# A woven graph-attention layer: VectorE adds up all three products of every slot group from the 22nd tile on, and two hand-set pacings are taken out

## The chip, the cores and the metric

The kernel runs on one core of a Trainium2 chip. The metric is device time in microseconds of one execution, from the median of several. Before the change it is 1743.26 us (three runs, 1741.64 to 1750.56 us). All profile lines below come from one profiled execution, whose own run took 1741.64 us and whose trace spans 1739.8 us from the first to the last instruction; the granted TensorE clock was 0.985 of full speed over that span.

## What is computed

One layer of graph attention over 4096 nodes with 512 features and 8 heads of 64, followed by a feed-forward block and a last layer norm. The mask is an adjacency matrix in which a node has some 17 neighbours, so nearly all of the 4096 x 4096 scores are masked out.

```python
hs, ht = layer_norm(x), layer_norm(h_target)
q = (ht @ Wq + bq).reshape(T, H, HD) / sqrt(HD)
k, v = (hs @ Wk + bk), (hs @ Wv + bv)            # per head
logits = where(adj != 0, q . k, -1e30)
ctx = softmax(logits) @ v
ht = layer_norm(ht + ctx @ Wo + bo)
out = layer_norm(x + ht + gelu(ht @ W1) @ W2)
```

Everything is float32. `adj` is 4096 x 4096 int32.

## The kernel before

**Preparation (to about 280 us).** K and V of all nodes are computed and written to one table in HBM (`kvd`, 1024 numbers per node). VectorE and ScalarE turn the rows of `adj` into lists of neighbours. The nodes are then sorted by their number of neighbours, in two halves, so that a tile of 128 nodes has nodes of about the same count.

**Tiles and slot groups.** There are 32 tiles. A tile's cap (11 to 39) is the largest number of neighbours that a node of it has. The caps in the order of the work are 11, 13, 14, 15, 15, 16, 17, 17, 18, 19, 19, 20, 22, 23, 24, 39, 12, 38, 13, 24, 14, 23, 15, 22, 15, 20, 16, 19, 17, 18, 17, 18: "tile 21" is the 22nd of them. Each neighbour position is a slot. Slots are worked on three at a time (`S = 3`); three slots are a full slot group, and a tile may end in a smaller one. 211 groups in all.

**One slot group.** GpSimd issues one gather per slot from `kvd` (L994) into a ring of 20 slots. VectorE multiplies the keys with the query (L1287) and sums by head (L1293). ScalarE takes the exponential (L1300, L1315) and multiplies the third slot's v with its weight, head by head (L1265, L1268). VectorE multiplies the first two slots' v with their weights (L1234). From tile 9 on it adds the second product to the first (L1238), and from tile 21 on (`DENSE = 21`) it also adds the third, but only in every other full group, by `j0 // S % 2` (L1241). What has not been added up goes to TensorE slot by slot: four 128x128 transposes per slot (L1247), which accumulate the context in PSUM (`cps`). So a slot added up by VectorE is four transposes less.

**A tile's tail.** `finish(i, ...)` is a generator that `advance()` steps twice per slot group. It sums the weights, takes the reciprocal, lets ScalarE spread it (L1133), TensorE transpose it (L1139), VectorE scale the context (L1144), TensorE add the residual (L1153) and multiply with Wo (L1157), and then goes through the layer norm to the transposed `h2T` (L1188, L1192). Between these stand `yield`s, whose number is set by `slow`: with `slow = 0` one step lies between L1144 and L1157, with `slow = 1` four. `slow` is 1 for tiles 7 to 10.

**A tile's front.** Gather of `h_target`, normalisation, transposes (L1037), query product (L1047), then VectorE's scaling of the query (L1052).

**Feed-forward.** `feed(g)` works on pairs of tiles (18 groups; the first three and the last are single tiles). It sleeps until `h2T` of its group is there, then goes through W1 (L1407), gelu (L1410) and W2 (L1416). `end` does the last norm, with rstd by GpSimd's pow (L692, called from `power`).

**The order of the work** is not left to a scheduler. `_weave` runs four generators (attention, the feeds, the second half's lists, weight loads), and always takes a piece from the one whose clock is lowest; a piece adds its cost in planner units to its clock. A pair of tiles costs 60 units in attention (`cost * n` twice per slot group) and 60 in the feed. `PACE` multiplies the cost of attention for some groups: 0.7 for tiles 1 to 4, 0.85 for tiles 5 to 8, 0.9 for tiles 9 and 10, and 1.1 for tiles 11 to 18. Every engine then works in the order in which its instructions were laid down.

Of the kernel before, what the change touches and what calls it, by code (L numbers as in the profile page):

```python
# [443 lines left out]
def adj_resnorm_kernel(  # L444
# [58 lines left out]
    S = 3  # L503
# [29 lines left out]
    with tc.tile_pool(name="keep", bufs=1) as keep:  # L533
# [17 lines left out]
        with ExitStack() as late:  # L551
# [171 lines left out]
            def behind(ins):  # L723
                return tc.issue_after(ins[-1]) if ins else nullcontext()
# [349 lines left out]
            def step(gens, i):  # L1074

                if i in gens and next(gens[i], StopIteration) is StopIteration:
                    del gens[i]

            def request(k):


                while issued[0] <= min(k + AHEAD, len(SG) - 1):
                    issue(issued[0])
                    mine = set(range(place[issued[0]], place[issued[0]] + SG[issued[0]][2]))
                    for m in range(max(k - len(held_up), 0), issued[0]):
                        assert not mine & set(range(place[m], place[m] + SG[m][2]))
                    issued[0] += 1
# [28 lines left out]
            def finish(i, p, cps, group, hs, mv):  # L1116


                rec, tq, cap = recs[i], tqs.pop(i), TILES[i][1]
                slow = 0 if i < QUICK or i > 10 else 1  # L1120
                first = i == 0

                nc.vector.scalar_tensor_tensor(p[:, :cap, :], rec[:, E0:E0 + cap].unsqueeze(2)
# [72 lines left out]
            def go_on():  # L1196
                for i in list(fronts):
                    step(fronts, i)
# [18 lines left out]
            def attention():  # L1217


                tails, pend, turns = [], [], []  # L1220

                def advance():
                    go_on()
                    for t in list(tails):
                        if next(t, StopIteration) is StopIteration:
                            tails.remove(t)

                def values(i, j0, n, kv, p, cps, after):

                    m = n - 1 if n == S else n
                    v4 = kv[:, :m, D:].rearrange("p j (h d) -> p j h d", h=H)
                    nc.vector.tensor_tensor(v4, v4, p[:, j0:j0 + m, :].unsqueeze(3)  # L1234
                                            .to_broadcast([P, m, H, HD]), ALU.mult)
                    slots = list(range(n))
                    if m > 1 and i >= ADDS and TILES[i][1] < (HEAVY if i > NA else 23):
                        nc.vector.tensor_add(kv[:, 0, D:], kv[:, 0, D:], kv[:, 1, D:])  # L1238
                        slots.remove(1)
                        if n == S and i >= DENSE and j0 // S % 2:  # L1240
                            nc.vector.tensor_add(kv[:, 0, D:], kv[:, 0, D:], kv[:, S - 1, D:])  # L1241
                            slots.remove(S - 1)

                    def turn():
                        for j in slots:
                            for c in range(KC):
                                nc.tensor.matmul(cps[:, c, :], kv[:, j, D + c * P:D + (c + 1) * P],  # L1247
                                                 ident, is_transpose=True,
                                                 start=j0 + j == 0 and c == 0,
                                                 stop=j0 + n == TILES[i][1] and j == slots[-1],  # L1250
                                                 skip_group_check=True)
                        if after is not None:
                            tails.append(after)

                    turns.append(turn)
                    held_up[:] = turns

                def add_up():
                    while turns:
                        turns.pop(0)()  # L1260
                    held_up.clear()

                def by_scalar(kv, lg):
                    pa = sp.tile([P, H], F32, name="pa")
                    nc.scalar.activation(pa, lg[:, S - 1, :], AF.Exp)  # L1265
                    for hd in range(H):
                        v = kv[:, S - 1, D + hd * HD:D + (hd + 1) * HD]
                        newest[:] = [nc.scalar.mul(v, v, pa[:, hd:hd + 1]).ins]  # L1268

                request(0)  # L1270
                yield 0.0
                k = 0
                for group in GROUPS:
                    hs = []
                    mv = sp.tile([P, 2, 2], F32, name="mv2")
                    cost = 0.5 * UNIT * len(group) / 2 / sum(TILES[i][1] for i in group)
                    if 0 < group[0] < 19:
                        cost *= PACE[(group[0] > 4) + (group[0] > 8) + (group[0] > 10)]
                    for i in group:
                        cps = ps.tile([P, KC, P], F32, name="cps", bufs=2)  # L1280
                        while k < len(SG) and SG[k][0] == i:
                            _, j0, n = SG[k]
                            while i not in tqs:
                                step(fronts, i)
                            kv, tq = kvs.pop(k), tqs[i]
                            with behind(closing[:1 if j0 < 2 * S else 2]):
                                nc.vector.tensor_tensor(kv[:, :n, :D], kv[:, :n, :D],  # L1287
                                                        tq[:, :D].unsqueeze(1)
                                                        .to_broadcast([P, n, D]), ALU.mult)
                            lg = sp.tile([P, S, H], F32, name="lg")  # L1290
                            latest[:] = [lg[:, 0, 0:1]]
                            with behind(closing if j0 == S else []):
                                logits[:] = [nc.vector.tensor_reduce(  # L1293
                                    lg[:, :n, :],
                                    kv[:, :n, :D].rearrange("p j (h d) -> p j h d", h=H),
                                    AX.X, ALU.add).ins]
                            if i != 1:
                                closing.clear()
                            if j0 > 0:
                                nc.scalar.activation(p[:, j0:j0 + n, :], lg[:, :n, :], AF.Exp)  # L1300
                            add_up()
                            if k > 0:
                                request(k - 1)
                            advance()
                            yield cost * n
                            if pend:
                                values(*pend.pop())
                                if i < QUICK:
                                    add_up()
                                if i < QUICK or i > NA:  # L1310
                                    request(k)
                            advance()
                            if j0 == 0:
                                p = sp.tile([P, MAXE, H], F32, name="p", bufs=1)
                                nc.scalar.activation(p[:, :n, :], lg[:, :n, :], AF.Exp)  # L1315
                            if n == S:
                                by_scalar(kv, lg)
                            last = j0 + n == TILES[i][1]
                            after = finish(i, p, cps, group, hs, mv) if last else None
                            pend.append((i, j0, n, kv, p, cps, after))  # L1320
                            yield cost * n
                            k += 1
                values(*pend.pop())
                add_up()
                while tails:
                    advance()
                    yield 3.0
                verdict()
# [138 lines left out]
            DENSE = 21  # L1467
            QUICK = 7
            UNIT = 60.0
            PACE = (0.7, 0.85, 0.9, 1.1)  # L1470

            ed = all_edges()
            steps = 2 * NQ + 1
# [41 lines left out]
            def fill():  # L1515
# [4 lines left out]
                for cost in _take(ed, FILL * steps):  # L1520
                    yield cost

            att = attention()
            _weave((projections(), 0), (prepare(), 0), (fill(), 0))
            src.close()
# [58 lines left out]
```

## Time and profile before

| what | value |
|---|---|
| median of 3 runs | 1743.26 us |
| the profiled execution, its own time | 1741.64 us |
| its span in the trace | 1739.8 us |
| TensorE (PE) busy | 1654.6 us, 95% |
| VectorE (DVE) busy | 1421.7 us, 82% |
| ScalarE (ACT) busy | 1236.4 us, 71% |
| GpSimd (POOL) busy | 994.5 us, 57% |
| first key product (L1287) of tile 0, 10, 21, 31 | 282.6, 646.5, 1183.2, 1600.2 us |
| last Wo product (L1157) ends | about 1658 us |

The page gives busy time by engine. A row of waits says which instruction of an engine was waiting for which other one, the microseconds in total, how often and the longest. A table of stretches gives each engine's busy time between two moments, and the clock granted to TensorE. A timeline row has start, length, engine, line, operation, out<-in, shape and count, and in brackets the idle time before it.

### The profile page before, as it was taken

What the parts mean: (1) busy time and instruction counts of PE and PEld (TensorE: products, weight loads), DVE (VectorE), ACT (ScalarE), POOL (GpSimd) and SP (SyncE); (2) the same over time, 40 slices, a digit from 0 to 9 for tenths busy, and PEclk for the clock granted to TensorE, in tenths of its full rate; (3) what the DMA queues carried; (4) which work ended last, traced back from release to release, by engine and by line L of the source; (5) the groups of instructions that cost most, each with busy time, mean ns of one, the idle gap of its engine ahead of it and who ended that gap; (6) DMA issues with size and microseconds to landing.
All of it is one profiled execution on the core that took longest, in us unless ns stands there. A gap on an engine that the chain in (4) does not pass through costs nothing. (4 is left out here: it accounts for less than half of the span.)

```text
span 1739.8 us, 22750 instructions
## 1 busy us (share of the span) xinstructions
PE 1654.6 (95%) x6994; PEld 1075.0 (62%) x6994; DVE 1421.7 (82%) x2450; ACT 1236.4 (71%) x3136; POOL 994.5 (57%) x824
## 2 busy tenths in 40 slices
PE   7999897899999999998999999999999999999997
PEld 3444444677676766665667677666656666666665
DVE  6887797889898999987778898898988879898700
ACT  5776674679678878786767877696877777686711
POOL 1000155666566685687777777777776776767101
PEclk9999998899999999999999999999999999999999
DMA  9999988978888898677788788778776777776100
GB/s 357 376 381 359 360 275 294 360 259 299 291 286 296 311 338 288 227 239 235 262 289 276 272 290 306 258 265 271 271 237 222 264 234 261 237 264 218 42 1 27
DMA packets 141611, 461.02 MB, mean 265 GB/s; under 512 B 18036, under 2 KB 23048, under 8 KB 141480
## 3 DMA queue, kind: packets, MB, share of 16 engines
q0 software_dynamic: 96272, 342.33, 58.0%
q1 hardware_dynamic: 39504, 98.26, 15.9%
q10 hardware_dynamic: 5704, 18.89, 2.7%
q8 instruction: 58, 0.95, 0.2%
q14 instruction: 73, 0.60, 0.1%
HBM read 430.61 MB, written 28.79 MB: 264 GB/s over the span
## 5 line engine op out<-in xcount | busy, mean ns | idle before, releaser
L994 POOL DMA_INDIRECT kv<-kvd,rec x603 | 775.9, 1287 | 320.9 <-issue 115.3
L1407 PE MATMUL pf<-h2T,w 128*128 128x256 f32 (+1 forms) x2304 | 471.3, 359 | 7.8 <-ACT h2T L1192 7.7
L1416 PE MATMUL po<-w,gt 128*128 128x512 f32 x1024 | 461.1, 593 | 1.4 <-ACT gt L1410 1.4
L1407 PEld LDWEIGHTS pf<-h2T,w 128*128 128x128 f32 x2304 | 394.1, 192 | 64.9 <-ACT h2T L1192 12.5
L1268 ACT ACTIVATE kv<-kv,pa 128x64 f32<-128x64 f32 x1520 | 392.0, 336 | 4.1
L1287 DVE TENSOR_TENSOR kv<-kv,tq 128x1536 f32<-128x1536 f32 (+2 forms) x211 | 351.4, 1676 | 51.8 <-DMA kv<-kvd,rec 40.8
L1293 DVE TENSOR_REDUCE lg<-kv 128x24 f32<-128x1536 f32 (+2 forms) x211 | 349.8, 1666 | 0.5
L1416 PEld LDWEIGHTS po<-w,gt 128*128 128x128 f32 x1024 | 187.3, 190 | 194.4 <-issue 190.8
L1247 PEld LDWEIGHTS cps<-ident,kv 128*128 128x128 f32 x1844 | 216.2, 142 | 89.7 <-issue 51.3
L1234 DVE TENSOR_TENSOR kv<-kv,p 128x1024 f32<-128x1024 f32 (+1 forms) x211 | 250.8, 1192 | 23.9 <-ACT p L1300 23.9
L1247 PE MATMUL cps<-ident,kv 128*128 128x128 f32 x1844 | 242.1, 276 | 17.5 <-DVE kv L1234 10.4
L692 POOL TENSOR_TENSOR n_rs<-n_ve,mhalf 128x2 f32<-128x2 f32 (+2 forms) x53 | 48.5, 915 | 313.4 <-DVE n_ve L685 170.7
L740 ACT ACTIVATE kv<-kv 128x1024 uint8<-128x1024 int32 x128 | 134.4, 1053 | 57.6 <-DMA kv<-in_adj_dram 21.7
L1410 ACT ACTIVATE gt<-pf 128x512 f32<-128x512 f32 x128 | 76.4, 597 | 98.1 <-PE pf L1407 96.9
L1410 ACT ACT_TABLE_LOAD x109 | 139.8, 1283 | 1.8
L1157 PE MATMUL t<-wo,rb 128*128 128x512 f32 x256 | 123.8, 629 | 12.5 <-DVE rb L1144 12.5
L956 PE MATMUL pq<-wv,h2T 128*128 128x512 f32 x256 | 115.7, 595 | 7.7 <-ACT kv L958 4.7
L956 PE MATMUL pq<-wk,h2T 128*128 128x512 f32 x256 | 118.0, 604 | 1.9 <-ACT tq L958 1.0
L1047 PE MATMUL t<-wq,tq 128*128 128x512 f32 x256 | 116.6, 600 | 0.7 <-ACT tq L1040 0.7
L749 DVE MAX8 cand<-kv 128x8 uint16<-128x171 uint16 (+1 forms) x384 | 108.0, 324 | 1.0
L1300 ACT ACTIVATE p<-lg 128x24 f32<-128x24 f32 (+2 forms) x179 | 39.0, 218 | 89.8 <-DVE lg L1293 86.6
L956 PEld LDWEIGHTS pq<-wv,h2T 128*128 128x128 f32 x256 | 48.1, 190 | 71.0 <-issue 57.2
(165 smaller groups left out, 1577.5 us busy)
## 6 DMA issues: line engine op xcount, KB each, us to landing
kv<-in_adj_dram SPq DMA_DIRECT2D x128, 512.0 KB, 7.1
kvd<-tq ACTq DMA_DIRECT2D x23, 512.0 KB, 7.4
kv<-kvd,rec POOLq DMA_INDIRECT x603, 5.8
kv<-in_L_gnn_h_target_dram SPq DMA_DIRECT2D x32, 256.0 KB, 6.6
w<-in_L_gnn_W_dram SPq DMA_DIRECT2D x8, 1024.0 KB, 9.8
kv<-in_x_dram SPq DMA_DIRECT2D x15, 512.0 KB, 7.9
kvd<-kv ACTq DMA_DIRECT2D x9, 512.0 KB, 6.1
rest_d<-gid SPq DMA_DIRECT2D x32, 96.0 KB, 5.4
```

The costliest lines, as they stand in the source:

```text
L740: nc.scalar.activation(sg, a, AF.Sign, accum_out=dpart[:, i, h:h + 1])
L956: nc.tensor.matmul(pkv, hT[:, kc, j * P:(j + 1) * P], w[:, kc, :], start=kc == 0, stop=kc == KC - 1)
L994: issues[:] = [nc.gpsimd.indirect_dma_start(out=dst, out_offset=None, in_=table[:, :], in_offset=bass.IndirectOffsetOnAxis(ap=idx, axis=0) ...
L1157: nc.tensor.matmul(pa, ct[:, c, :], wo[:, c, :], start=False, stop=c == KC - 1, skip_group_check=True)
L1234: nc.vector.tensor_tensor(v4, v4, p[:, j0:j0 + m, :].unsqueeze(3) .to_broadcast([P, m, H, HD]), ALU.mult)
L1247: nc.tensor.matmul(cps[:, c, :], kv[:, j, D + c * P:D + (c + 1) * P], ident, is_transpose=True, start=j0 + j == 0 and c == 0, stop=j0 + n ...
L1268: newest[:] = [nc.scalar.mul(v, v, pa[:, hd:hd + 1]).ins]
L1287: nc.vector.tensor_tensor(kv[:, :n, :D], kv[:, :n, :D], tq[:, :D].unsqueeze(1) .to_broadcast([P, n, D]), ALU.mult)
L1293: logits[:] = [nc.vector.tensor_reduce(lg[:, :n, :], kv[:, :n, :D].rearrange("p j (h d) -> p j h d", h=H), AX.X, ALU.add).ins]
L1407: nc.tensor.matmul(pf[:, k, :], w1[(f0 + k) // KC][:, kc, (f0 + k) % KC * P:((f0 + k) % KC + 1) * P], h2T[:, kc, :w], start=kc == 0, stop= ...
L1410: nc.scalar.activation(gt, pf, AF.Gelu_apprx_tanh)
L1416: nc.tensor.matmul(po[j], gt[:, k, j * P:(j + 1) * P], w2[(f0 + k) // KC][:, (f0 + k) % KC, :], start=False, stop=f0 + k == FC - 1, skip_g ...
```

## The change

Three edits:

1. `slow` is 1 for every tile from 7 on, not for tiles 7 to 10 alone. Tiles 11 to 31 get one step more ahead of the transposes of the spread reciprocal, one ahead of L1144, three ahead of L1157, and one ahead of the transposes of `h` (L1188).
2. From tile 21 on, the third product is added by VectorE (L1241) in every full slot group, not in every other one.
3. `PACE` ends at tile 8: tiles 9 and 10 cost 1.0 instead of 0.9 of their units, tiles 11 to 18 cost 1.0 instead of 1.1.

```diff
-                slow = 0 if i < QUICK or i > 10 else 1
+                slow = 0 if i < QUICK else 1
...
-                        if n == S and i >= DENSE and j0 // S % 2:
+                        if n == S and i >= DENSE:
                             nc.vector.tensor_add(kv[:, 0, D:], kv[:, 0, D:], kv[:, S - 1, D:])
                             slots.remove(S - 1)
...
-                    if 0 < group[0] < 19:
-                        cost *= PACE[(group[0] > 4) + (group[0] > 8) + (group[0] > 10)]
+                    if 0 < group[0] < 9:
+                        cost *= PACE[group[0] > 4]
...
-            PACE = (0.7, 0.85, 0.9, 1.1)
+            PACE = (0.7, 0.85)
```

## The prediction, made before the changed kernel had run

> **What bounds the kernel now.** I read the page's busy times first, then TensorE's waits from 350 us (where attention and feed are both under way) to 1640 us, then busy time by stretch, then VectorE's waits in the late stretch. The chain that ended last covers only the final 3 us and tells nothing. The page:
>
> ```profile
> span 1739.8 us, 22750 instructions
> ...
> PE 1654.6 (95%) x6994; PEld 1075.0 (62%) x6994; DVE 1421.7 (82%) x2450; ACT 1236.4 (71%) x3136; POOL 994.5 (57%) x824
> ```
>
> TensorE is the bound on the whole, VectorE is second. The costliest of TensorE's waits from 350 to 1640 us (total, times, longest):
>
> ```profile
> PE t L1157 <- DVE rb L1144: 12.5, 3, 6.0
> PE pf L1407 <- ACT h2T L1192: 7.7, 6, 2.4
> PE cps L1247 <- DVE kv L1238: 7.1, 9, 1.7
> ```
>
> Everything listed there comes to 34 us. So a saving must be work taken from TensorE or one of these few waits. Busy time by stretch (columns: PE, weight loads, DVE, ACT, POOL, clock, DMA share, GB/s):
>
> ```profile
> 646.00:735.00 89.00, 83.63 (x370) 56.74 (x369) 88.86 (x142) 70.39 (x182) 57.49 (x47) 1.00 0.79 273
> 735.00:1230.00 495.00, 479.55 (x2176) 330.35 (x2175) 423.09 (x456) 374.63 (x1022) 370.13 (x296) 0.99 0.80 268
> 1230.00:1640.00 410.00, 402.07 (x1659) 265.57 (x1658) 360.70 (x449) 304.34 (x806) 269.93 (x203) 1.00 0.68 227
> ```
>
> The second number is the length. VectorE is the bound only from 646 to 735 us (88.86 of 89.00), and there TensorE idles 5.4 us. Late, where the added work goes, VectorE has 410.0 - 360.7 = 49.3 us free. What it waits for there:
>
> ```profile
> DVE tq L1052 <- PE t L1047: 33.9, 8, 8.4
> DVE n_nm L697 <- POOL n_rs L692: 11.6, 5, 4.7
> DVE n_nm L1373 <- POOL n_rs L692: 1.3, 2, 0.9
> ```
>
> 33.9 us are waits for TensorE itself, which vanish as soon as VectorE is the later one. Its own waits are 11.6 + 1.3 and about 1 us more: 14.
>
> **The third product (edit 2).** In tiles 21 to 31 the full groups number 7, 5, 7, 5, 6, 5, 6, 5, 6, 5, 6; the even ones, new to L1241, are 4, 3, 4 and eight times 3: 35. The instruction orders of the two programs agree: L1241 28 before, 63 after; L1247 1844 and 1704. TensorE loses 140 transposes. Their price is not the row's mean of 276 ns, since they overlap: in the timeline a row of twelve starts at 442.12 and the next line at 443.43, 0.109 us each. 140 x 0.109 = 15.3 us. The matching VectorE row, 128x512, takes 0.68 us, but the next instruction starts 0.60 after (1459.13 to 1459.73): 35 x 0.60 = 21 us.
>
> The Trainium skill, TensorE: Matmul & The Clock Gate, Part 4: PE-mode transpose, gives about 275 ns for a transpose in a kernel's context, as the row does (276 ns). As a price per transpose it would make the saving an estimated 38.5 us; the starts in the trace decide for 15.3.
>
> 31 of the 35 adds fall into the late stretch. TensorE would need 410.0 - 31 x 4 x 0.109 = 396.5 us, VectorE 360.7 + 31 x 0.60 + 14 = 393.3. That is a margin of 3 us where there were 35: a tie. The best end is -15.3. The other end takes VectorE's share from 735 to 1230 us, 423.09/495 = 85.5%, as its limit: 379.3/0.855 = 444 us, +34. Nearest is the stretch 646 to 735, where VectorE was late and still lost nothing; but with a tie the two wait for each other now and then. I take **-11**.
>
> GpSimd issues the gathers. In the timeline one issue beside a reduce took 0.94 us (1454.66) and one beside a two-operand multiply 1.68 (1456.67). If each new add held GpSimd for its whole 0.68 us, that is 35 x 0.68 = 24 us of GpSimd's time, of which it has 410 - 270 = 140 free late. Nothing on the path; without that cover gathers would land late and L1287 wait.
>
> The Trainium skill, SBUF — State Buffer, SBUF: two separate sides, speaks against the edit: a VectorE instruction with two SBUF inputs and a GpSimd one that reads SBUF lock each other out entirely. The two issues above agree; by the rule the 24 us would be lost to GpSimd in full, by the rows at most that.
>
> **The longer tails (edit 1).** L1157 stood waiting for L1144 at 461, 807 and 912 us; the last two are tiles 12 and 14, which get three more steps between the two:
>
> ```profile
> 800.12 0.60 PE L1153 MATMUL t<-ident,tq 128*128 128x128 f32 x4
> 806.70 6.36 PE L1157 MATMUL t<-wo,rb 128*128 128x512 f32 x8 [5.98 <-DVE rb L1144]
> 812.90 1.47 PE L1247 MATMUL cps<-ident,kv 128*128 128x128 f32 x12
> ```
>
> These eight rows took 6.36 us instead of the 3.60 of a row at full clock: the wait costs twice. At 912 us it is 2.93 us, and seven rows of 4.72 instead of 7/8 x 3.60. Together 5.98 + 2.93 + 2.76 + 1.57 = 13.2 us. What is late next: three steps are one and a half slot groups, some 9 us (tile 12 has eight groups and starts 50.3 us ahead of tile 13, 6.3 us a group), more than the longest of these waits. Price between -13.2 and 0 (VectorE later by as much); I take **-13**. The steps also make `h2T` later, by six, which is the other half of the feed's wait (7.7 us now).
>
> **The pace (edit 3).** Counting each program's order with the start-to-start times, TensorE has 17.6 us less to do ahead of tile 18's first transposes and 11.6 less ahead of tile 21's, as feed work moves behind attention; that work returns at the end at its own price. What can cost: VectorE from 735 to 1230 us. TensorE would need 495 - 13 - 12 = 470; VectorE is busy 423 and idle 72, of which 17.9 for TensorE (L1052), 27.9 for gathers, 16.7 for exponentials. If all but the 17.9 is its own, it needs 477: +7. In tile 11 (691 to 735, VectorE 100% busy) some 3 us of feed are missing: +3. In tile 10 there is more feed to fill TensorE's 3.1 us of idle: -2. So -2 to +10; I take **+4**, between them, since part of the gather waits are TensorE's lateness in releasing slots.
>
> **The feed's sleep.** Walking the planner's costs: before, the feed sleeps once, at 554.9 to 560.7 units (tile 19), and the trace shows 1.0 us of TensorE idle there (1131 us). After, it runs on, and sleeps at 854.9 to 862.7 (tile 29): 7.8 units, in which TensorE has attention alone. A pair's feed is 128 x 0.216 + 64 x 0.429 = 55 us for 60 units, so 7.8 units are 7.2 us. Between 0 and +7.2; **+3**, as VectorE has little lead there now.
>
> Sum: -11 - 13 + 4 + 3 = -17. The profiled execution took 1741.64 (span 1739.8 and 1.8 around it), 1.6 below the median of 1743.26: **1725 us**.
>
> **Rivals.**
> *All of it comes through:* -15.3 - 13.2 - 2 + 0 = -30: 1711 us. For it: VectorE without a gap from 646 to 735. Against: the tie.
> *No gain, VectorE takes over late:* its gather waits of 735 to 1230 come back (27.9/495 x 410 = 23 us) on top of the 14: 379.3 + 37 = 416, +6; then +6 - 13 + 4 + 3 = 0: 1742 us. For it: gathers wait for TensorE's transposes to release slots (112 us of GpSimd's idle time in the whole run). Against: no gather wait in the late stretch today.
> *Slower:* one mechanism, VectorE's queue from tile 21 on held at the 85.5% of the middle stretch: 444 us, +34 - 13 + 4 + 3 = +28: 1769 us. It decides once the late stretch needs over 410 + 15 us, that is VectorE under 379/425 = 89% busy there. For it: five long in-order instructions per group with an exponential and a gather in the loop, and only 3 us of margin. Against: its waits late are nearly all for TensorE.
>
> **How the numbers follow.** About 0.5% (8.7 us) is what a measurement of this kernel can tell from no change. Forecast 0.50, the -30 case 0.08, no gain 0.25, slower 0.17. So faster 0.58, same 0.25, slower 0.17. The range 1710 to 1752 takes in all but the slower case. The forecast's own range is 1711 to 1734.
>
> **What would show it.** Right: L1241 x63, L1247 x1704; L1157's wait left only at 461 us; L1052's late wait for TensorE down from 33.9 to under 15; VectorE over 93% busy in the late stretch, that stretch some 10 us shorter. Wrong: TensorE's wait at L1247 for L1241 or L1234 over 20 us; VectorE waiting for gathers or exponentials after tile 21; idle TensorE at tile 29, or from tile 11 to 19, over 15 us.

## The result, and the profile after

The change makes the kernel a little slower: the ratio to before is **1.0039** (95% interval 1.0023 to 1.0056). The medians over 22 runs each are 1753.67 us after and 1746.65 us before. That is inside the 0.5% which the prediction called "no change", but clear of the noise and on the other side of the forecast of 1725 us (-1.05% against 1743.26).

The page after has the same shape as before, with less work on TensorE and 12 us more span:

```profile
span 1751.5 us, 22533 instructions
...
PE 1642.4 (94%) x6854; PEld 1059.7 (61%) x6854; DVE 1440.1 (82%) x2485; ACT 1236.7 (71%) x3136; POOL 1042.8 (60%) x824
```

TensorE is busy 12.2 us less (1654.6 before), with 140 matmuls less, as counted. GpSimd (POOL) is busy 48 us more, with the same 824 instructions; 20 us of that lie in the late stretch, where 31 of the 35 new adds are. Busy time by stretch, in the columns of before:

```profile
646.00:735.00 89.00, 84.83 (x369) 56.68 (x368) 88.79 (x146) 70.21 (x185) 66.80 (x46) 1.00 0.78 263
735.00:1230.00 495.00, 470.94 (x2119) 324.92 (x2118) 425.44 (x457) 361.33 (x1004) 383.30 (x297) 0.98 0.81 270
1230.00:1640.00 410.00, 390.75 (x1544) 252.88 (x1543) 377.70 (x486) 317.25 (x817) 289.83 (x206) 0.99 0.70 230
```

In the middle and late stretches (735 to 1230 us and 1230 to 1640 us) TensorE is busy 9 and 11 us less than before in the same time: work was taken away, and idle time stands in its place. What VectorE waits for from 1230 to 1640 us:

```profile
DVE n_nm L697 <- POOL n_rs L692: 22.2, 5, 9.9
DVE tq L1052 <- PE t L1047: 3.8, 1, 3.8
```

The wait for TensorE fell from 33.9 to 3.8 us, as foretold. But the wait for GpSimd's pow, taken as fixed, doubled (11.6 before). The longest, 9.9 us, shows how. First VectorE:

```profile
1385.35 0.26 DVE L685 TENSOR_SCALAR n_ve<-mv 128x2 f32<-128x2 f32 x1
...
1386.38 0.44 DVE L1126 TENSOR_REDUCE sums<-p 128x8 f32<-128x160 f32 x1
1396.68 0.16 DVE L697 SCALAR_TENSOR_TENSOR n_nm<-mv,n_rs 128x2 f32<-128x2 f32 x1 [9.86 <-POOL n_rs L692]
```

Then GpSimd, which has to make `n_rs` from the `n_ve` that is ready at 1385.6:

```profile
1376.80 3.59 POOL L994 DMA_INDIRECT kv<-kvd,rec  x1 [0.30 <-issue]
1380.69 3.69 POOL L994 DMA_INDIRECT kv<-kvd,rec  x1 [0.30 <-DMA kv<-kvd,rec]
1384.68 0.94 POOL L994 DMA_INDIRECT kv<-kvd,rec  x1 [0.30 <-issue]
...
1394.94 0.94 POOL L994 DMA_INDIRECT kv<-kvd,rec  x1 [0.30 <-issue]
1395.90 0.74 POOL L692 TENSOR_TENSOR n_rs<-n_ve,mhalf 128x2 f32<-128x2 f32 x1
```

Pow stands in GpSimd's queue behind nine gathers, 1.25 us from start to start. By the rows some 5.4 of the 9.86 us come from the two issues before them, which took 3.6 us apiece instead of 0.94. Both began while VectorE ran instructions with two inputs in SBUF (all below but the reduce, L1293), and ended 0.8 us after the last of a row of these (at 1380.39 and 1384.38):

```profile
1376.62 1.22 DVE L1234 TENSOR_TENSOR kv<-kv,p 128x1024 f32<-128x1024 f32 x1
1377.76 1.22 DVE L1287 TENSOR_TENSOR kv<-kv,tq 128x1024 f32<-128x1024 f32 x1
1378.89 0.68 DVE L1238 TENSOR_TENSOR kv<-kv 128x512 f32<-128x512 f32 x1
1379.49 1.21 DVE L1293 TENSOR_REDUCE lg<-kv 128x16 f32<-128x1024 f32 x1
1380.62 0.68 DVE L1241 TENSOR_TENSOR kv<-kv 128x512 f32<-128x512 f32 x1
1381.22 2.35 DVE L1234 TENSOR_TENSOR kv<-kv,p 128x1024 f32<-128x1024 f32 x2
```

Over the whole profile before, a gather of `kv` that began while VectorE ran L1293's reduce took 0.95 us in the mean (178 of them, the longest 1.01), beside an idle VectorE 0.94 (88), and beside a product of L1234 or L1287 of over 1 us 1.82 (225).

VectorE, in order, stands behind pow, and its key products come 10 us late. ScalarE makes `h` at once, and TensorE transposes it by 1399.4. But ScalarE then has to go through the exponentials of the late slot groups before it comes to `h2T`:

```profile
1396.88 1.52 ACT L1179 ACTIVATE h<-h,n_nm,n_rs 128x512 f32<-128x512 f32 x2 [10.47 <-DVE n_nm L697]
1402.87 0.22 ACT L1315 ACTIVATE p<-lg 128x24 f32<-128x24 f32 x1 [2.67 <-DVE lg L1293]
1404.53 0.22 ACT L1300 ACTIVATE p<-lg 128x24 f32<-128x24 f32 x1 [1.34 <-DVE lg L1293]
1406.57 1.91 ACT L1192 ACTIVATE h2T<-t,cols 128x256 f32<-128x256 f32 x4
```

So the feed, and TensorE with it, waits for `h2T`:

```profile
1407.17 5.20 PE L1407 MATMUL pf<-h2T,w 128*128 128x256 f32 x14 [7.74 <-ACT h2T L1192]
```

In the middle stretch the two waits of L1157 are gone, and these of TensorE are new (735 to 1230 us):

```profile
PE cps L1247 <- DVE kv L1234: 6.5, 2, 5.6
PE t L1037 <- ACT tq L1033: 6.3, 2, 6.1
PE t L1188 <- ACT h L1179: 4.4, 4, 3.2
```

**Where the time went, as a sum.** From the first key product of tile 9 (ahead of it the two profiles differ by 2.7 us) to the last matmul I split TensorE's time into its work (each row at the start-to-start time of its shape at full clock), idle times over 0.3 us, what rows took longer while the granted clock was at half, and a small rest:

| kernel | work | idle | half clock | rest |
|---|---|---|---|---|
| before | 1084.2 | 29.2 | 6.4 | 8.9 |
| after | 1068.9 | 46.7 | 11.6 | 10.2 |

-15.3 + 17.5 + 5.2 + 1.3 = +8.7 us. The work went as predicted to the tenth; idle time and the half clock that follows it more than took its place. TensorE idles 10.3 us more in tiles 11 to 18 (24.3 against 14.0) and 11.0 more in tiles 21 to 30 (18.8 against 7.8), and a little less elsewhere.

### The profile page after: what moved, and what is told of

Same layout as the page of the kernel before. It is cut to its first block, busy times and chain, and to the rows that moved or that the text cites. A ratio compares the mean times of both kernels' runs of the same rounds, so it can differ in the third digit from the quotient of the medians.

```text
span 1751.5 us, 22533 instructions
## 1 busy us (share of the span) xinstructions
PE 1642.4 (94%) x6854; PEld 1059.7 (61%) x6854; DVE 1440.1 (82%) x2485; ACT 1236.7 (71%) x3136; POOL 1042.8 (60%) x824
## 5 line engine op out<-in xcount | busy, mean ns | idle before, releaser
L994 POOL DMA_INDIRECT kv<-kvd,rec x603 | 805.0, 1335 | 277.4 <-issue 116.0
L1287 DVE TENSOR_TENSOR kv<-kv,tq 128x1536 f32<-128x1536 f32 (+2 forms) x211 | 351.9, 1675 | 67.9 <-DMA kv<-kvd,rec 61.0
L1293 DVE TENSOR_REDUCE lg<-kv 128x24 f32<-128x1536 f32 (+2 forms) x211 | 350.4, 1666 | 0.3
L1247 PEld LDWEIGHTS cps<-ident,kv 128*128 128x128 f32 x1704 | 200.6, 143 | 101.9 <-issue 42.1
L1234 DVE TENSOR_TENSOR kv<-kv,p 128x1024 f32<-128x1024 f32 (+1 forms) x211 | 250.8, 1192 | 11.0 <-ACT p L1300 10.3
L1247 PE MATMUL cps<-ident,kv 128*128 128x128 f32 x1704 | 227.4, 277 | 30.9 <-DVE kv L1234 17.7
L692 POOL TENSOR_TENSOR n_rs<-n_ve,mhalf 128x2 f32<-128x2 f32 (+2 forms) x53 | 55.8, 1053 | 324.7 <-DVE n_ve L685 157.6
L1157 PE MATMUL t<-wo,rb 128*128 128x512 f32 x256 | 119.2, 609 | 6.6 <-DVE rb L1144 6.6
L1047 PE MATMUL t<-wq,tq 128*128 128x512 f32 x256 | 118.6, 607 | 2.9 <-ACT tq L1040 2.9
## 6 DMA issues: line engine op xcount, KB each, us to landing
w<-in_L_gnn_W_dram SPq DMA_DIRECT2D x8, 1024.0 KB, 10.2
```

Of the source, the lines that this page charges most:

```text
L994: issues[:] = [nc.gpsimd.indirect_dma_start(out=dst, out_offset=None, in_=table[:, :], in_offset=bass.IndirectOffsetOnAxis(ap=idx, axis=0) ...
L1157: nc.tensor.matmul(pa, ct[:, c, :], wo[:, c, :], start=False, stop=c == KC - 1, skip_group_check=True)
L1287: nc.vector.tensor_tensor(kv[:, :n, :D], kv[:, :n, :D], tq[:, :D].unsqueeze(1) .to_broadcast([P, n, D]), ALU.mult)
L1293: logits[:] = [nc.vector.tensor_reduce(lg[:, :n, :], kv[:, :n, :D].rearrange("p j (h d) -> p j h d", h=H), AX.X, ALU.add).ins]
```

## The experiments

Each ratio is to runs of the kernel before on the same chip in the same set, with its 95% interval. The sets differ: the median of the kernel before was 1757 us in that of edits 1, 2, 3 and of 1 and 3, and 1745 to 1750 us in the others. So up to some 10 us between single profiles of different sets come from the set and not from the edit. All edits are on the kernel before unless it says otherwise.

### The three edits, alone and in pairs

Edit 2 alone (`if n == S and i >= DENSE:`):

> Edit 2 alone (every full group of tiles 21 to 31 adds its third product on VectorE; slow and PACE as before). Theory A (GpSimd is the hidden second bound: the new two-operand adds lengthen its gather issues, its queue runs late, and VectorE waits in the late stretch for GpSimd's pow, so the 15.3 us taken from TensorE come back only in part): ratio to before 0.995 to 1.000, VectorE's wait for n_rs in 1230 to 1640 us over 15 us against 13. Theory B (edit 2 is worth its -11 as predicted, and the loss is all in the middle, from edits 1 and 3): ratio 0.992 to 0.995. Theory C (VectorE late costs more than TensorE saves): ratio over 1.003.

Edit 1 alone (`slow = 0 if i < QUICK else 1`):

> Edit 1 alone (slow = 1 from tile 7 on). The waits of L1157 at 807 and 912 us should go. Theory A: the tail's later steps fall on other waits, the gain stays under half of 13 us: ratio 0.997 to 1.003. Theory B: the h2T that comes six steps later makes the feed sleep more, slower: 1.003 to 1.008. The prediction's own step: 0.992 to 0.994.

Edit 3 alone (`PACE = (0.7, 0.85)`, up to tile 8):

> Edit 3 alone (no 0.9 for tiles 9 and 10, no 1.1 for tiles 11 to 18). Theory A (attention ahead of its gathers: VectorE waits for gathers and TensorE for VectorE between 735 and 1230 us, over 10 us more than before): ratio 1.004 to 1.009. Prediction's step (+4 us): 1.001 to 1.004. Rival (nothing): 0.999 to 1.001.

Edits 1 and 3:

> Edits 1 and 3 without edit 2. If the edits add up, this is the sum of the two alone. Theory A (the loss lies in the middle stretch and edit 2 only hides part of it): 1.006 to 1.012, slower than the changed kernel's 1.0039. Theory C (edit 2 is the loss): under 1.002.

Edits 1 and 2:

> Edits 1 and 2 without edit 3 (PACE as before). If edit 3 is the loss in the whole change (1.0039): 0.996 to 1.001. If the edits do not add up and every reweaving finds its own stalls: anything else, 1.002 or more.

| kernel | ratio | interval |
|---|---|---|
| edit 2 alone | 1.0016 | 0.9996 to 1.0036 |
| edit 1 alone | 0.9987 | 0.9972 to 1.0001 |
| edit 3 alone | 1.0059 | 1.0038 to 1.0079 |
| 1 and 3 | 1.0030 | 1.0014 to 1.0046 |
| 1 and 2 | 1.0063 | 1.0044 to 1.0083 |
| all three | 1.0039 | 1.0023 to 1.0056 |

No edit gains what it was given. They don't add up either: edit 3 costs 0.6% alone, and with the other two in place nothing can be seen of it (1.0063 to 1.0039). Edit 2 comes to +0.16% alone, +0.8% on edit 1, +0.1% on edits 1 and 3: nowhere the -0.6% of the prediction. Theory B of the first run (edit 2 is worth its 11 us) fell; 1.0016 does not decide between A (to 1.000) and C (over 1.003). Edits 1 and 3 together (1.0030) lie between the two theories that stood for them.

### Edit 2 taken apart

The third products left out, so that TensorE saves its transposes and VectorE pays nothing:

```diff
-                        if n == S and i >= DENSE and j0 // S % 2:
-                            nc.vector.tensor_add(kv[:, 0, D:], kv[:, 0, D:], kv[:, S - 1, D:])
+                        if n == S and i >= DENSE:
+                            if j0 // S % 2:
+                                nc.vector.tensor_add(kv[:, 0, D:], kv[:, 0, D:], kv[:, S - 1, D:])
                             slots.remove(S - 1)
```

> On the kernel before: the 35 third products of the even full groups of tiles 21 to 31 are left out altogether (neither added by VectorE nor transposed by TensorE), so TensorE has 140 transposes less and VectorE nothing more. If TensorE is the bound late, as predicted, this gains its 15.3 us: ratio 0.990 to 0.993. If TensorE's work there is not what sets the time, or stalls take its place: over 0.996.

The adds alone, into the used-up key half of slot 0 (`kv[:, 0, :D]`), with all transposes kept:

> On the kernel before: VectorE makes the 35 extra adds of edit 2, but into a place that nobody reads, and TensorE still transposes all that it did before. This is the price of the adds alone. Prediction's step (VectorE has 33 us of slack late, waits for TensorE): 0.999 to 1.002. If the adds cost in full because what looks like slack is not: 21 us, 1.010 to 1.013.

As edit 2, but with a reduce (one input) in place of each new add:

```diff
...
+                            else:
+                                scr = sp.tile([P, H], F32, name="scr", bufs=1)
+                                nc.vector.tensor_reduce(
+                                    scr, kv[:, S - 1, D:].rearrange("p (h d) -> p h d", h=H),
+                                    AX.X, ALU.add)
                             slots.remove(S - 1)
```

> As edit 2 alone, but the 35 new VectorE adds with two SBUF inputs are replaced by a reduce of the same 512 numbers (one input, about the same 0.67 us, result unused; the 35 third products are left out of the sum). If the two-input adds do their harm by holding up GpSimd's gather issues: clearly faster than edit 2 alone, near the run that drops the products. If it is VectorE's time: like edit 2 alone (1.000 to 1.003).

The kernel before, for a profile from the same set:

> The kernel before, unchanged, for a profile from the same chip as the other runs of this set. All theories: ratio 1; waits of L1157 for L1144 of 9 us between 735 and 1230 us.

It spans 1743.6 us, its instructions stand in the same order on every engine, and its waits are those of the first profile within 2 us: L1157 for L1144 8.9 us in the middle, 32.2 (33.9 there) for TensorE and 11.6 for pow late.

The two-input add into an unread place, with the transposes of the 35 products left out:

> On the kernel before: in tiles 21 to 31 the third products of the 35 even full groups are not transposed (TensorE saves 15.3 us), and VectorE makes a two-input add of the same size, but into a place that nobody reads, so that TensorE never waits for it (these 35 products are left out of the sum). Against the reduce run (0.9971) it differs in having two SBUF inputs, against edit 2 alone (1.0016) in that TensorE does not wait for the result. Theory port (two inputs hold up GpSimd): 1.000 to 1.003, GpSimd's gather issues longer than in the reduce run. Theory dependence (TensorE's wait for L1241 is the price): 0.996 to 0.998.

| kernel | ratio | interval |
|---|---|---|
| products dropped | 0.9942 | 0.9918 to 0.9965 |
| one-input reduce instead of the add | 0.9971 | 0.9953 to 0.9989 |
| edit 2 (two-input add, used) | 1.0016 | 0.9996 to 1.0036 |
| two-input add, unread, transposes out | 1.0024 | 1.0008 to 1.0041 |
| two-input add, unread, transposes kept | 1.0045 | 1.0026 to 1.0064 |

TensorE's saving is real: 0.58% of 1750 is 10 us of the 15.3. The adds cost more than that: from 0.9942 to 1.0016 is 0.74%, 13 us for 21 us of VectorE time that the prediction gave for 4. With all transposes kept the adds cost 0.45%, 8 us, between the two values expected. The unread add costs 0.8%, as much as the add that TensorE waits for, and in these two runs VectorE, ScalarE and GpSimd work through the same instructions in the same order. So the dependence is not the price. A reduce of the same length costs only 0.29%, which points to the two inputs. But with the reduce some 75 other instructions of VectorE, 60 of ScalarE and 20 of GpSimd also stand elsewhere in their order, so this pair alone doesn't show it; what shows the hold on GpSimd directly are the issue times of the section on the result. GpSimd's gathers (1230 to 1640 us, count, busy, mean ns, idle before) in the reduce run and in edit 2 alone:

```profile
L994 POOL DMA_INDIRECT kv<-kvd,rec x165 | 217.5, 1318 | 108.2 <-issue 34.4 <-PE cps L1253 26.6 <-DVE kv L1238 15.2
```

```profile
L994 POOL DMA_INDIRECT kv<-kvd,rec x170 | 235.4, 1385 | 106.2 <-issue 35.8 <-PE cps L1247 22.4 <-DVE kv L1238 18.5
```

1318 against 1385 ns: slower by 0.067 us x 170 = 11 us. The dropped run has 1319, the unread add 1356. But the control has 1387 without any new add, so the mean also moves with how the engines happen to lie; by itself it doesn't show what the adds cost.

### GpSimd's pow taken out of VectorE's path

A reciprocal on VectorE in place of pow, with the square root left out:

```diff
-                nc.gpsimd.tensor_tensor(rs, ve, mhalf[:, :n], ALU.pow)
+                if name == "n2":
+                    nc.vector.reciprocal(rs, ve)
+                else:
+                    nc.gpsimd.tensor_tensor(rs, ve, mhalf[:, :n], ALU.pow)
```

> On the kernel before: the rstd of the second layer norm (name n2, in the attention's tails) is made by a reciprocal on VectorE in place of GpSimd's pow, so the square root is left out there. VectorE then no longer waits for GpSimd's queue in the tails (12 us late, 3 us in the middle). If this wait is price on the path even before: 0.992 to 0.997. If VectorE's wait is covered by its slack: 0.998 to 1.002.

And on top of edit 2:

> Edit 2 alone with the same replacement (square root of n2 left out). Theory (GpSimd's queue, held up by two-input adds, makes VectorE wait for pow, and so edit 2's saving is lost): against the run above it should gain a good part of the 10 us that dropping the products gained: ratio to before 0.988 to 0.994, and below e13 by 0.004 or more. Rival (the add's own time and TensorE's wait for it are the price): equal to e13 or above it.

Measured: **0.9958** (0.9942 to 0.9974) without edit 2, **0.9911** (0.9892 to 0.9929) with it. So the wait for pow cost some 0.4% in the kernel before already. With pow out of the way edit 2 gains 0.47%, 8 us, where it gained nothing before: the stated 0.004, if only just. Half of what VectorE still waits for late is then TensorE again, a third is the last norm's pow, and TensorE hardly waits for `h2T` (edit 2 without pow, 1230 to 1640 us):

```profile
DVE tq L1055 <- PE t L1050: 9.8, 4, 4.4
DVE n_nm L1376 <- POOL n_rs L695: 6.1, 2, 5.4
```

```profile
PE cps L1250 <- DVE kv L1244: 4.7, 3, 2.7
PE pf L1410 <- ACT h2T L1195: 1.8, 3, 1.0
```

In edit 2 alone L1247's waits in that stretch were 20.0 us (11.2 with the unread add, in a faster set). TensorE's order is the same with pow and without it but for one instruction; some 75 of VectorE's and 85 of ScalarE's instructions moved. So the wait for pow is what edit 2's saving was lost to, as far as these runs go. The full norm on VectorE was to make it useful:

```diff
...
+                    nc.vector.tensor_single_scalar(yi, ve.bitcast(I32), 1,
+                                                   op=ALU.logical_shift_right)
+                    nc.vector.tensor_scalar(yi, yi, -1.0, 1597463007.0, op0=ALU.mult, op1=ALU.add)
+                    for _ in range(2):
+                        nc.vector.tensor_mul(t, rs, rs)
+                        nc.vector.scalar_tensor_tensor(t, t, -0.5, ve, op0=ALU.mult, op1=ALU.mult)
+                        nc.vector.scalar_tensor_tensor(rs, t, 1.5, rs, op0=ALU.add, op1=ALU.mult)
...
```

> Edit 2 alone, with n2's rstd computed in full on VectorE: a first guess by integer shift and subtraction and two Newton steps, eight small instructions in place of GpSimd's pow. By e14 (0.9911 with one instruction and without the square root) less seven small VectorE instructions of about 0.1 us for each of 18 groups (12 us of VectorE, part of it in slack): 0.991 to 0.998. If VectorE's own time is the price after all: over 1.000.

It is slower: 1.0079 (1.0053 to 1.0105). In its trace the eight small instructions don't stand together: the framework has put other VectorE work between them, and from the first to the last it takes 5.8 us in the mean (104 us over 18 groups). TensorE then waits 10.3 us for `h` from tile 9 on (L1188 in the code of before), 0.3 in the run with the reciprocal. That is the smaller part of the 1.7% between the two; the rest I can't place; TensorE's own order differs between them too. This also corrects what the section on the kernel before says: the weave sets the order in which work is laid down, but the order of VectorE, ScalarE and GpSimd is still moved about when an instruction is changed.

The same on the whole change:

> The whole change with the same rstd on VectorE as e16. VectorE waits 24 us late for pow in the changed kernel, TensorE 11 us for h2T behind it. If GpSimd's queue is also the whole change's loss: 0.994 to 0.999. If edit 3's stalls in the middle stretch stay: 1.000 to 1.004, between the changed kernel and before.

0.9984 (0.9965 to 1.0003), that is 0.55% faster than the changed kernel (1.0039). The late wait for pow in the tails is gone there too.

A later wait in place of another engine (for tiles 19 on, pow stays on GpSimd), on edit 2 alone:

```diff
                 rs = power(sp, mv[:, :nh, :], nh, "n2", ve)
                 yield
+                if i > 18:
+                    yield
                 nm = negmean(sp, mv[:, :nh, :], rs, nh, "n2")
```

> Edit 2 alone, with one step more between pow and the instruction of VectorE that waits for it (tiles 19 on), pow staying on GpSimd. If only VectorE's standing wait for pow matters: 0.995 to 1.000, and the wait for n_rs late down from 19 us to under 8. If the order of the work is what a step upsets, as with edit 1: 1.000 to 1.006.

**0.9924** (0.9900 to 0.9948), the fastest that computes everything, and faster than both kernels, and past the end of what was expected (0.995). What VectorE waits for from 1230 to 1640 us:

```profile
DVE n_nm L1375 <- POOL n_rs L692: 8.9, 4, 3.3
DVE tq L1052 <- PE t L1047: 5.1, 4, 2.4
```

The tails' wait for pow (L697, 14.7 us in edit 2 alone) is gone from this stretch. What is left is the last norm's (L1375), which the step doesn't touch and which grew from 2.2 us; with it the sum is 8.9, not the under 8 expected. The step also moves some 320 of TensorE's 6854 instructions, so not all of the gain need be this wait.

### The pacing and the tails, taken apart

Only the 1.1 taken out (`PACE = (0.7, 0.85, 0.9, 1.0)`):

> On the kernel before: PACE (0.7, 0.85, 0.9, 1.0), so only the 1.1 of tiles 11 to 18 is taken out. Edit 3 whole was 1.0059. Theory A (the middle stretch's attention cannot go faster than it does, so feed work moved out of it leaves TensorE idle there): 1.004 to 1.008, all of edit 3's loss. Rival (it is tiles 9 and 10 whose slower weaving delays all after): under 1.002.

1.0156 (1.0133 to 1.0180): more than the whole of edit 3. With tiles 9 and 10 at 0.9 attention enters the middle six planner units further ahead of the feed than in edit 3. TensorE's waits from 735 to 1230 us:

```profile
PE t L1157 <- DVE rb L1144: 7.5, 1, 7.5
PE cps L1247 <- DVE kv L1234: 7.4, 3, 6.0
PE t L1037 <- ACT tq L1033: 6.8, 1, 6.8
PE t L1188 <- ACT h L1179: 3.1, 1, 3.1
PE t L1047 <- ACT tq L1040: 2.9, 1, 2.9
```

From tile 9 to tile 21 TensorE has 537.4 us of work here against 554.9 in the control, and yet the time is longer (595.0 us against 586.1): attention did not go faster for the feed that was moved out, and more than all of it became idle time and half clock. Giving the feed more than before:

> On the kernel before: PACE (0.7, 0.85, 0.9, 1.2) for tiles 11 to 18. Theory A says that the middle stretch still has 20 us of TensorE idle that more feed would fill, as far as the feed is not used up: 0.993 to 0.999. Rival (1.1 is where VectorE and TensorE are level, and the feed now outruns h2T and sleeps): 0.999 to 1.006.

1.0023 (1.0002 to 1.0043), so 1.1 is near the best of these three. The 0.9 alone raised to 1.0 was not tried, so how much of edit 3 lies there stays open. The three waits of L1157 (tiles 4, 12, 14) removed by name:

```diff
-                slow = 0 if i < QUICK or i > 10 else 1
+                slow = 1 if i in (4, 7, 8, 9, 10, 12, 14) else 0
```

> On the kernel before: slow = 1 also for tiles 4, 12 and 14 alone, the three whose L1157 waits for L1144 (12.5 us in all), and for no other after 10. If a wait removed is time won: 12.5 us and some 7 of half clock, 0.989 to 0.994. If, as with edit 1 alone (0.9987), other waits take their place: 0.996 to 1.001.

1.0113 (1.0087 to 1.0139), slower than either theory had it. In the middle stretch L1157's wait falls to 0.6 us, but 14.2 us of feed that had stood ahead of tile 9 now stand behind it (work from tile 9 on 1099.2 against 1085.0), with 26.3 us more idle and half clock over the whole run.

The split of TensorE's time from tile 9 on, as in the first section:

| kernel | work | idle | half clock | rest |
|---|---|---|---|---|
| before, again | 1085.0 | 29.1 | 6.3 | 9.0 |
| edit 2 | 1068.9 | 50.2 | 16.3 | 9.2 |
| edit 1 | 1084.6 | 34.7 | 5.1 | 10.1 |
| edit 3 | 1084.6 | 39.0 | 12.8 | 8.2 |
| products dropped | 1068.5 | 33.8 | 10.2 | 9.0 |
| only the 1.1 out | 1084.6 | 49.2 | 18.3 | 10.8 |
| no pow in n2 | 1084.2 | 22.5 | 7.8 | 8.4 |
| no pow in n2, edit 2 | 1068.5 | 26.8 | 6.4 | 10.6 |
| one step later, edit 2 | 1068.9 | 33.7 | 10.8 | 8.9 |

Single profiles stray by some 0.3% from their medians, and the rows of edits 1, 2 and 3 come from the set in which the kernel before took 1757 us. So the rows are for seeing which column moves, and not by how much.

## Why the prediction was wrong, point by point

- **TensorE is the bound; so less work on it is less time.** Half right. The 15.3 us of work went exactly, and 10 us of them came through as time when VectorE had no adds to make for them (0.9942).
- **The adds cost 4 us, since VectorE's 49 us of free time late is mostly waiting for TensorE.** This is the step that failed for edit 2. Those waits did vanish (33.9 to 3.8), but the adds cost 13 us. The step took VectorE's "own waits" of 14 us as fixed, and they grew: pow's from 11.6 to 22.2 us in the whole change, and from 12.9 to 16.9 with the last norm's in edit 2 alone.
- **GpSimd: "nothing on the path", with 140 us free.** Wrong, and as far as the runs show the root of the step above. The amount was no surprise: "at most" 24 us were forecast, and GpSimd is busy 14 to 20 us longer late (289.8 us against 269.9 and 275.6 in the two profiles before; 286.6 in edit 2 alone). The two rows it was read from (0.94 us beside a reduce, 1.68 beside a two-operand multiply) were the right ones. The rule of the Trainium skill that was weighed there (SBUF — State Buffer, SBUF: two separate sides) spoke against the edit, and on GpSimd's side this case's trace agrees with it: issues took 1.82 us in the mean when they began beside a long two-input product and 0.95 beside a reduce. What was missed is that GpSimd's queue also holds pow, for which VectorE stands in order. A queue that is 70% busy need only be late for 10 us at that moment. Three results speak for pow as the way: the pair without it (0.47% gained), the step later (0.9924), and the whole change with the norm on VectorE (0.9984 against 1.0039). The norm in full on VectorE on edit 2 alone (1.0079) does not, and is explained only in part. Each of these edits also moves other instructions, so a share of each number may be that.
- **The longer tails: -13.** Wrong: -0.13% (-2 us) alone, +0.5% on edit 2. The two waits went, as foretold, and others took their place: in edit 1 alone TensorE waits 5.6 us for `h`, 9.5 for products and 3.4 for gelu in the middle stretch. "What is late next" asked about the same tile's chain only; the steps also move the feed, L1047 and L1188 of the neighbours.
- **The pace: +4.** Too small alone: +0.59%, 10 us, the upper end of the -2 to +10 that was given. Feed moved out of the middle left idle time: 28.7 us on TensorE in tiles 11 to 18 against 13.9. On top of the other two edits no cost of it can be seen.
- **The feed's sleep: +3.** Not there: in the profile after TensorE has no idle time over 0.3 us in tile 29. The 7.7 us wait for `h2T` is at 1407 us, behind pow.
- **The rivals.** "No gain, VectorE takes over late" gave the right size by the wrong wait: gathers are no late wait of VectorE (none in the list after), pow is. The "slower" case was not it: VectorE was at 377.7 of 410, 92%, over its 89%. Of the signs of being wrong one came: TensorE idles 24.3 us from tile 11 to 18, over the 15.
- **The sum.** Four terms were added as if each stood alone. The measured edits don't add up: edits 1 and 2 should make 1.0003 and gave 1.0063, and all three should make 1.0062 and gave 1.0039.

Open: why edit 3 costs nothing on top of the other two, and where the norm in full on VectorE loses its last 1%.

## What to carry to other kernels

Ask of each engine with free time not how much it has but what else stands in its queue, and who waits in order for that: a small instruction behind a row of gathers can turn an engine that is 70% busy into the path. Where one order was tuned by hand, a wait taken away comes back somewhere else; test such edits one at a time, and let no sum of them be a forecast. A step put between a small producer and its in-order consumer costs one line, and here it turned an edit that gained nothing into a gain of 0.8%, some of which may be the new order that it brings.

## What the runs showed of the hardware

An idle time of some 3 us or more on TensorE was mostly followed by its granted clock at half. In the profile after, from 350 us on, all five idle times of 3.2 to 7.7 us were (for 6.8 us from 462, 800, 875 and 1046 us, 10.2 us from 1401), and one of five of 2.2 to 2.7 us (3.4 us from 964). In edit 1 alone one of 3.4 us at 1047 us was not. What rows lost by it from tile 9 on comes on top of the idle time, a seventh to a good third of it (5.1 to 34.7 us in edit 1, 6.3 to 29.1 in the control, 18.3 to 49.2 with only the 1.1 out).

A gather issued by GpSimd took 0.95 us when it began beside a reduce of VectorE, and 1.82 us in the mean beside a long instruction with two inputs in SBUF (profile before, 178 and 225 gathers). At equal length on VectorE (0.68 us), 35 unread instructions with two inputs gave 1.0024 and 35 with a single one 0.9971; the order of other instructions differs too between these two.
